# Table casts moved from VectorE to GpSimd, and a third group of keys put ahead of the quantiser's maximum

## The chip, the cores and the metric

The kernel runs on one core of a Trainium2 chip. Its five engines work side by side, each through its own instructions in order, and wait for each other by semaphores: TensorE (PE: matmuls and transposes; PEld is its loading of weights), VectorE (DVE), ScalarE (ACT), GpSimd (POOL) and SyncE (SP, which here only issues transfers). The metric is the device time of one execution in microseconds (us). Before the change it is 1597.74 us, the median of three runs (1596.93 to 1598.61).

## The reference

The program is two layers of a transformer on `x` of shape (2, 2048, 512), with a context of 128 tokens per batch, all in float32. Each layer is a cross attention and a feed-forward, both behind a normalisation and both added to `x`:

```python
x = x + _L0_xattn_ref(_layernorm(x), ctx_1024, ctx_1024, mask_BxS2_bf0, ...)
x = x + _L0_ffn_ref(_layernorm(x), clip_x, clip_down, w_gate, w_up, w_down)
x = x + _L1_xattn_ref(_layernorm(x), ctx_1024, ctx_1024, mask_1x1xSxS2_bk0, Wq, bq, Wk, bk, ...)
x = x + _L1_ffn_ref(_layernorm(x), Wg, bg, We, be)
```

The change lies where the first feed-forward begins. That feed-forward quantises its input with a single step for the whole tensor, and the step needs the largest absolute value over all tokens:

```python
def _act_fake_quant(x, clip_factor):
    scale = jax.nn.sigmoid(clip_factor) * jnp.max(jnp.abs(x)) / QMAX
    return jnp.clip(_ste_round(x / scale), -QMAX - 1.0, QMAX) * scale

xq = _act_fake_quant(x, clip_x[0])
gate = jnp.einsum('bsh,ih->bsi', xq, _weight_fake_quant(w_gate))
up = jnp.einsum('bsh,ih->bsi', xq, _weight_fake_quant(w_up))
h = _act_fake_quant(jax.nn.silu(gate) * up, clip_down[0])
return jnp.einsum('bsi,hi->bsh', h, _weight_fake_quant(w_down))
```

So no row of the feed-forward can be quantised before the attention has finished its last tile. The second attention projects keys and values from the context alone (`K = k @ Wk.T + bk`), so its keys don't depend on `x` and can be computed at any time. Its queries are `Q = q @ Wq.T + bq`, divided by the square root of the head's width. The second feed-forward is a mixture of eight experts, where each token goes to the one expert that its gate picks.

## The kernel before

The 4096 tokens are 32 tiles of 128 tokens (`NT`), one tile per SBUF buffer `x0` to `x31`, which hold the residual from beginning to end.

The first attention walks blocks of 256 tokens, with the order of the work on TensorE, VectorE, ScalarE and GpSimd written out by hand. At its end `finished` (line 456) adds a tile's attention to the residual, takes the mean and variance and has GpSimd raise the variance to the power of -0.5 (`rsqrt_eps`, line 101), which gives `rstd1`; `largest` (line 464) normalises the tile with it (`xn`, line 104) and takes the largest absolute value per row (line 468). The last two tiles, 30 and 31, go through this in sequence, and the maximum of tile 31 is the last thing that the quantiser waits for.

From line 572 on TensorE's order alone is kept as written; VectorE, ScalarE, GpSimd and SyncE are put in order by a planner that works with its own costs, so that instructions of this stage can come between the last ones of the attention. The planner's queue per engine is then fixed, and each engine runs it strictly in order.

The seam, lines 593 to 717, does these things:

- `table` (line 593) makes small tables of ascending numbers for the routing of the experts at the very end: GpSimd writes integers with `iota` into a shared buffer `ti`, and line 598 casts them into the table's own type. Five tables, of 8, 128, 24, 32 and 1 numbers per partition, go through the one buffer `ti`, each waiting for the cast of the one before. Beside them stand the fills of `before`, `onesb` and the first row of `cum`, and a select on GpSimd that makes `before` triangular.
- `keys` (line 658) computes one of four groups of the second attention's keys: four matmuls of `wk1` and the turned context into PSUM (two passes each in the profile, so eight records per group), and ScalarE's copy with the bias. `psm` has two PSUM buffers for this stage.
- `act_step` (line 620) makes the quantiser's step: VectorE's maximum `m` and its spread `mb`, TensorE's transpose `pm` (line 628), VectorE's `gm`, then `step`, `inv` and the scales `gsc`, `rsx`, `usc`.
- `quantised_x` (line 694) writes a tile as int8 (`xi`) and casts it to bf16 (`xq`); there are two buffers for the first and four for the second. `turned_x` (line 700) turns the first four tiles with TensorE's transposes (`ptx`) and ScalarE's copies, and all later ones with transposing DMAs on SyncE's queue.
- Lines 716 and 717 fill `ones1` (read by nobody) and divide the query bias `bq`; lines 720 to 736 load and combine rows for the gate's bias (`vrow`, `wrow`, `rowadd`), and GpSimd adds `rowadd` to the gate's weights at line 736.

The feed-forward (line 738) then runs eight blocks of 512 tokens by eleven slices of the hidden width. A slice is four matmuls into `pg` and four into `pu`, `gate` on ScalarE, the product `h` (line 752) and its maximum `hmax` (line 754) on VectorE, and the store of `h` to DRAM on SyncE (line 755). `pg` and `pu` have three PSUM buffers each, so TensorE starts the fourth `pu` when the first `h` is done. The tiles of the next block are quantised and turned along the way.

After that the down projection (lines 1211 to 1230) takes tile by tile: a matmul group `py`, VectorE's product `y`, and GpSimd's addition into the residual (line 813). The query bias is read at line 875, from the 25th of these iterations on.

Of the kernel before, what the change touches and what calls it, by code (L numbers as in the profile page):

```python
# [19 lines left out]
ALU = mybir.AluOpType  # L20
# [6 lines left out]
ND = D // P  # L27
# [6 lines left out]
H1, DH1 = 16, 32  # L34
# [29 lines left out]
def two_layers(ctx: ExitStack, tc: tile.TileContext, a, out):  # L64
    nc = tc.nc
# [85 lines left out]
    with ExitStack() as l0:  # L151
# [96 lines left out]
        def keys(g):  # L248

            pk = psm.tile([P, 2, B * T], F32, name="pk", tag="m")  # L250
            for par in range(2):
                for c in range(ND):
                    nc.tensor.matmul(
                        pk[:, par, :], wk[g][c // 2][:, c % 2, par, :], kvT[c // 2][:, c % 2, :], start=(c == 0), stop=(c == ND - 1)
                    )
            t = []
            for k, (par, tab) in enumerate(((0, cosk), (1, sink), (1, cosk), (0, sink))):
                t.append(turns_k[k // 2][:, k % 2])
                nc.vector.tensor_tensor(
                    t[k], pk[:, par, :].rearrange("p (b k) -> p b k", b=B),  # L260
                    tab.unsqueeze(1).to_broadcast([P, B, T]), ALU.mult,
                )
            nc.gpsimd.tensor_tensor(kTe[:, g, :].rearrange("p (b k) -> p b k", b=B), t[0], t[1], ALU.subtract)
            nc.gpsimd.tensor_tensor(kTo[:, g, :].rearrange("p (b k) -> p b k", b=B), t[2], t[3], ALU.add)
# [42 lines left out]
        def down(w, j):  # L307
            wb = quantised(w, sd[:, j : j + 1])

            def turn():  # L310
                nc.sync.dma_start(out=wdT[:, :, j * P : (j + 1) * P], in_=wb, transpose=True)

            return turn
# [14 lines left out]
        def normed(k):  # L328


            stats[k] = small.tile([P, NB0, 2], F32, name="stat")
            for t, n in enumerate(tiles[k]):
                mv = variance(xs[n])
                ve = small.tile([P, 1], F32, name="ve")
                nc.vector.tensor_scalar(ve, mv[:, 1:2], 1.0 + EPS, EPS * EPS, ALU.mult, ALU.add)
                nc.vector.tensor_copy(stats[k][:, t, 0:1], mv[:, 0:1])
                nc.gpsimd.tensor_tensor(stats[k][:, t, 1:2], ve, minus_half, ALU.pow)
            if k > 1:
                features_in(k)
                turned_in(k)  # L340
# [42 lines left out]
        def queries(u, par):  # L383

            k, g = divmod(u, NG)
            j, b = blocks[k]
            if par == 0:
                if j not in tabs:
                    tables_in(j)
                ropes[u] = [mid.tile([P, B0], F32, name=f"rt{i}", bufs=1) for i in range(4)]  # L390
            pq, rt = psm.tile([P, B0], F32, name="pq", tag="m"), ropes[u]
            for c in range(ND):
                nc.tensor.matmul(  # L393
                    pq, wqs[c // 2][:, c % 2, par, g * P : (g + 1) * P], xnTs[k][:, c, :], start=(c == 0), stop=(c == ND - 1)
                )
            cos, sin = tabs[j]
            if par == 0:
                nc.vector.tensor_tensor(rt[0], pq, cos, ALU.mult)  # L398
                nc.vector.tensor_tensor(rt[1], pq, sin, ALU.mult)
                return  # L400
            qs[u] = [mid.tile([P, B0], F32, name=f"q{i}") for i in range(2)]
            nc.vector.tensor_tensor(rt[2], pq, sin, ALU.mult)  # L402
            nc.gpsimd.tensor_tensor(qs[u][0], rt[0], rt[2], ALU.subtract)  # L403
            nc.vector.tensor_tensor(rt[3], pq, cos, ALU.mult)
            nc.gpsimd.tensor_tensor(qs[u][1], rt[3], rt[1], ALU.add)
# [181 lines left out]
    bq = wa.tile([P, ND], F32, name="bq")  # L587
    bob = wa.tile([P, D], F32, name="bob")
    masks = wa.tile([P, TPB, T], U8, name="masks")
    ones1 = wa.tile([P, DH1], F32, name="ones1")  # L590


    def table(shape, pattern, base=0, channel=0, dtype=BF16):
        ti = w1.tile([P, *shape], I32, name="ti", tag="ti")
        nc.gpsimd.iota(ti, pattern=pattern, base=base, channel_multiplier=channel)
        t = w1.tile([P, *shape], dtype, name=f"t{len(tables)}")
        tables.append(t)
        nc.vector.tensor_copy(t, ti)
        return t

    tables = []
    iota_e = table([NE], [[1, NE]], dtype=F32)
    iota_s = table([P], [[1, P]])
    iota_j = table([NJB], [[1, NJB]], dtype=F32)
# [1 line left out]
    iota_p = table([1], [[0, 1]], channel=1, dtype=F32)  # L606

    before = w1.tile([P, P], BF16, name="before")
    nc.vector.memset(before, 1.0)
    nc.gpsimd.affine_select(  # L610
        out=before, in_=before, pattern=[[1, P]], compare_op=ALU.is_ge, fill=0.0, base=-1, channel_multiplier=-1
    )
    onesb = w1.tile([P, P], BF16, name="onesb")
    nc.vector.memset(onesb, 1.0)
    hot = w1.tile([P, NT, NE], BF16, name="hot")

    cum = w1.tile([P, NT + 1, NE], BF16, name="cum")
    nc.vector.memset(cum[:, 0, :], 0.0)

    def act_step(psum, name, column_maxima):  # L620

        m = small.tile([P, 1], F32, name="m")
        nc.vector.tensor_reduce(m, column_maxima, AX.X, ALU.max)

        mb = small.tile([P, P], F32, name="mb", bufs=1)
        nc.vector.tensor_copy(mb, m.to_broadcast([P, P]))
        pm = psum.tile([P, P], F32, name="pm", tag="m")
        nc.tensor.transpose(pm, mb, ident)
        gm = small.tile([P, 1], F32, name="gm")
        nc.vector.tensor_reduce(gm, pm, AX.X, ALU.max)  # L630
        step = const.tile([P, 1], F32, name=f"step_{name}")
        nc.vector.tensor_scalar(step, gm, kept[name], 1.0 / QMAX, ALU.mult, ALU.mult)
        inv = const.tile([P, 1], F32, name=f"inv_{name}")
        nc.vector.reciprocal(inv, step)
        return step, inv

    with ExitStack() as up:
# [38 lines left out]

            return rest

        for f in range(2):
            keys(f)  # L680
        sx, isx = act_step(psm, "L0_ffn_clip_x", amax1)
        for f in range(2, ND):
            keys(f)
        rsx = kv.tile([P, NT], F32, name="rsx")
        nc.vector.tensor_scalar(rsx, rstd1, isx, None, ALU.mult)
        gsc = kv.tile([P, NI], F32, name="gsc")
# [13 lines left out]
        def turned_x(n):  # L700
            blk, t = divmod(n, NBF)
            if t == 0:
                xqTs[blk] = work.tile([P, ND, BF], BF16, name="xqT", bufs=2)
            if blk > 0:
                nc.sync.dma_start(out=xqTs[blk][:, :, t * P : (t + 1) * P], in_=xqs[n], transpose=True)
                return
            pt = psm.tile([P, ND, P], BF16, name="ptx", tag="m")
            for c in range(ND):
                nc.tensor.transpose(pt[:, c, :], xqs[n][:, c * P : (c + 1) * P], identb)
            nc.scalar.copy(xqTs[blk][:, :, t * P : (t + 1) * P], pt)  # L710
# [2 lines left out]
            quantised_x(n)  # L713
        for n in range(NBF):
            turned_x(n)
        nc.vector.memset(ones1, 1.0)
        nc.vector.tensor_scalar(bq, bq, 1.0 / math.sqrt(DH1), None, ALU.mult)


        nq = (NE + 1) * ND  # L720
# [17 lines left out]
        for blk in range(NT // NBF):  # L738
            for i in range(NI):
# [19 lines left out]
                t, odd = divmod(i, 2)  # L759
                n = (blk + 1) * NBF + t  # L760
# [3 lines left out]
                if i >= 3 and i % 2 == 1:  # L764
                    n = (blk + 1) * NBF + (i - 3) // 2
# [27 lines left out]
    def rounded(n):  # L793

        if 0 < n < NT:
            h = work.tile([P, NI, P], F32, name="hq", bufs=3)
            load(h, h_dram[n])
            his[n] = work.tile([P, NI, P], I8, name="hi")
            nc.scalar.activation(his[n], h, AF.Identity, scale=ish)

    def widened(n):
        if n < NT:
            hbs[n] = work.tile([P, NI, P], BF16, name="hb")
            nc.vector.tensor_copy(hbs[n], his[n])
# [49 lines left out]
    def turned1(n):  # L854

        blk, t = divmod(n, NB1)
        if t == 0:
            xTs[blk] = big.tile([P, ND, B1], F32, name="xT1")
        dst = xTs[blk][:, :, t * P : (t + 1) * P]
        if n >= TURNED:  # L860
            joined(dst, xn1s[n])
        else:
            nc.scalar.copy(dst, transposed(psm, xn1s[n]))
# [347 lines left out]
    for n in range(NT - held):  # L1211
        rounded(n + 2)
        widened(n + 1)
        for rest in rests:
            rest()
        down(n)
        rests = []
        if n == NT - held - 6:
            rests = [normed(t) for t in range(NB1)]
        if n == NT - held - 5:  # L1220
            for t in range(NB1):
                turned1(t)
        if n >= NT - held - 4:
            f = n - NT + held + 4
            queries(0, range(f, f + 1))
        if n == NT - held - 2:
            rests = [normed(NB1 + t) for t in range(NB1)]
        if n == NT - held - 1:
            for t in range(NB1):
                turned1(NB1 + t)  # L1230
# [5 lines left out]
    for n in range(NT):  # L1236
        blk, t = n // NB1, n % NB1
# [138 lines left out]
```

## Time and profile before

| What | Value |
|---|---|
| median of three runs | 1597.74 us (1596.93 to 1598.61) |
| the profiled execution's own time | 1599.43 us |
| its span, first to last instruction | 1597.4 us |
| TensorE busy | 1551.3 us, 97% of the span |
| VectorE, ScalarE, GpSimd busy | 75%, 45%, 37% |
| mean granted clock of TensorE | 0.995 |

Busy shares alone don't say what the seam costs, as it is 12 us of 1597. What does is the order of its instructions in time and the idle times between them. In the rows of the timeline the first number is the start in us from the span's beginning, the second the duration; then come the engine, the line, the operation with what it writes and reads, the shape, and the number of instructions; in brackets stand the engine's idle time just before and what ended it. In the table of waits the numbers behind the colon are the total in us, how often, and the longest.

By such rows the seam lies between 673 us, when the last tile's attention is added, and 686.5 us, when the first `pg` starts; the feed-forward's first two blocks end at about 726 us.

### The profile page before, as it was taken

The page shows a single profiled execution, that of the slowest core. Times are in us where ns is not written, and L with a number is a line of the kernel's source. Part 1 is how long each engine was busy: PE and PEld are TensorE (multiplying, and loading weights), DVE is VectorE, ACT ScalarE, POOL GpSimd, SP SyncE. Part 2 cuts the span into 40 slices and gives each one's busy share as a digit, 9 for nine tenths or more (in the row PEclk, how much of TensorE's full clock was granted, in tenths as well). Part 3 has the DMA queues.
Part 4 walks back from the last instruction along what each step waited for, and adds up shares of the span by engine and source line. Part 5 has one row for each costly group of instructions (what it writes and reads, how often), then busy time and mean ns, then how long its engine had stood idle before and what let it go on. Part 6 is the DMA issues. An engine that isn't in the chain of part 4 may idle for free. (4 is left out here: it accounts for less than half of the span.)

```text
span 1597.4 us, 26167 instructions
## 1 busy us (share of the span) xinstructions
PE 1551.3 (97%) x9542; PEld 909.1 (57%) x9542; DVE 1192.5 (75%) x2333; ACT 720.4 (45%) x1537; POOL 586.8 (37%) x580
## 2 busy tenths in 40 slices
PE   7999999999999999999999999999999999999997
PEld 5655555555555555544444466666666666654443
DVE  3467777777777886589986678888888888877442
ACT  1222222222222222243335566777777776763442
POOL 2232222222222222110005654555565444544553
PEclk9999999999999999999999999999999999999999
DMA  9511212111111220367768734221311111114553
GB/s 321 188 37 41 47 40 47 40 47 40 51 46 41 59 60 1 117 169 205 179 173 278 271 132 143 48 47 34 55 45 36 41 28 41 41 47 131 162 162 89
DMA packets 180571, 150.90 MB, mean 94 GB/s; under 512 B 97089, under 2 KB 144665, under 8 KB 180444
## 3 DMA queue, kind: packets, MB, share of 16 engines
q1 hardware_dynamic: 170188, 127.25, 28.5%
q0 software_dynamic: 6240, 18.70, 3.8%
q10 hardware_dynamic: 4016, 3.29, 0.9%
q8 instruction: 76, 1.25, 0.3%
q14 instruction: 51, 0.42, 0.1%
HBM read 89.97 MB, written 41.79 MB: 82 GB/s over the span
## 5 line engine op out<-in xcount | busy, mean ns | idle before, releaser
L419 ACT ACTIVATE pr<-sc 128x1024 f32<-128x1024 f32 x64 | 65.6, 1024 | 421.6 <-PE sc L414 421.4
L393 PE MATMUL pq<-xnT,wq 128*128 128x256 f32 x1024 | 254.4, 391 | 0.0
L451 PE MATMUL pw<-wo,att 128*128 128x512 f32 x512 | 230.8, 593 | 0.0
L393 PEld LDWEIGHTS pq<-xnT,wq 128*128 128x128 f32 x1024 | 184.4, 189 | 67.1 <-issue 44.0
L914 ACT ACTIVATE s<-s,mx 128x128 f32<-128x128 f32 x512 | 175.3, 388 | 28.1 <-DVE mx L905 28.1
L923 POOL TENSOR_TENSOR s<-s,rs 128x1024 f32<-128x1024 f32 x64 | 120.9, 1903 | 149.6 <-DVE rs L922 149.1
L403 POOL TENSOR_TENSOR q<-rt,rt 128x256 f32<-128x256 f32 x64 | 46.7, 730 | 339.7 <-DVE rt L402 335.2
L451 PEld LDWEIGHTS pw<-wo,att 128*128 128x128 f32 x512 | 96.9, 190 | 96.4 <-issue 89.9
L441 DVE RECIPROCAL rd<-sc 128x256 f32<-128x256 f32 x64 | 112.4, 1757 | 46.5 <-PE sc L435 46.5
L1195 PE MATMUL pz<-we,x 128*128 x312 | 139.3, 598 | 1.8 <-ACT x L832 1.6
L872 PE MATMUL pq<-xT,wq 128*128 128x256 f32 x512 | 122.6, 382 | 0.0
L978 PE MATMUL pl<-wgate,xnT 128*128 128x512 f32 x256 | 116.7, 599 | 0.0
L955 PE MATMUL pw<-wo,oT 128*128 128x512 f32 x256 | 115.2, 592 | 0.7 <-ACT oT L946 0.7
L872 PEld LDWEIGHTS pq<-xT,wq 128*128 128x128 f32 x512 | 96.0, 190 | 33.1 <-issue 20.3
L398 DVE TENSOR_TENSOR rt<-pq,rope_cos 128x256 f32<-128x256 f32 x64 | 27.0, 422 | 104.2 <-PE pq L393 104.2
L749 ACT ACTIVATE gate<-pg,gsc 128x512 f32<-128x512 f32 x88 | 60.5, 687 | 93.9 <-PE pg L744 84.0
L1195 PEld LDWEIGHTS pz<-we,x 128*128 128x128 f32 x312 | 58.2, 192 | 68.4 <-issue 65.2
L92 DVE BATCH_NORM_STATS2 st<-x 128x6 f32<-128x512 f32 x130 | 89.4, 688 | 6.0 <-DMA x<-in_ctx 3.8
L744 PE MATMUL pu<-xqT,wuT 128*128 128x512 bf16 x352 | 90.3, 379 | 2.6 <-DVE h L752 2.4
L744 PE MATMUL pg<-xqT,wgT 128*128 128x512 bf16 x352 | 90.3, 379 | 0.0
L900 DVE SCALAR_TENSOR_TENSOR s<-sc,keep 128x1024 f32<-128x1024 f32 x64 | 78.1, 1220 | 14.3 <-PE sc L892 9.1
L955 PEld LDWEIGHTS pw<-wo,oT 128*128 128x128 f32 x256 | 48.6, 190 | 55.3 <-issue 53.6
(226 smaller groups left out, 2811.8 us busy)
## 6 DMA issues: line engine op xcount, KB each, us to landing
h_dram<-h SPq DMA_DIRECT2D x88, 256.0 KB
hq<-h_dram SPq DMA_DIRECT2D x31, 704.0 KB
x_dram<-x SPq DMA_DIRECT2D x32, 258.0 KB
x<-in_x SPq DMA_DIRECT2D x32, 256.0 KB
we<-in_L_ffn_We SPq DMA_DIRECT2D x8, 1024.0 KB
xnT<-in_x_turned SPq DMA_DIRECT2D x14, 512.0 KB
along<-stat_dram SPq DMA_DIRECT2D x14, 256.0 KB
w_in<-in_L_ffn_w_gate SPq DMA_DIRECT2D x11, 256.0 KB
```

The lines of the kernel that those rows point to most:

```text
L92: nc.vector.bn_stats(out=st, in_=x)
L393: nc.tensor.matmul(pq, wqs[c // 2][:, c % 2, par, g * P : (g + 1) * P], xnTs[k][:, c, :], start=(c == 0), stop=(c == ND - 1))
L441: nc.vector.reciprocal(rd, sc[:, 0, B0:])
L451: nc.tensor.matmul(pw, atts[u][:, f, t * P : (t + 1) * P], wo[:, 2 * g + f, :], start=(g == 0 and f == 0), stop=(g == NG - 1 and f == 1),)
L744: nc.tensor.matmul(dst, w[:, c, i * P : (i + 1) * P], xqTs[blk][:, c, :], start=(c == 0), stop=(c == ND - 1),)
L872: nc.tensor.matmul(pq, wq1[:, c, f * P : (f + 1) * P], xTs[blk][:, c, :], start=(c == 0), stop=(c == ND - 1))
L900: nc.vector.scalar_tensor_tensor(s, sc[:, 2 * half : 2 * half + 2].rearrange("p r c k -> p (r c) k"), -MASKED, keeps[n].unsqueeze(1).to_br ...
L914: nc.scalar.activation(s[:, h, :], s[:, h, :], AF.Exp, bias=mx[:, h : h + 1], **accum)
L923: nc.gpsimd.tensor_tensor(s, s, rs.unsqueeze(2).to_broadcast([P, 8, T]), ALU.mult)
L955: nc.tensor.matmul(pw, os_[n][:, c, :], wo1[:, c, :], start=(c == 0), stop=(c == ND - 1))
L978: nc.tensor.matmul(pl, xn2T[n][:, c, :], wgate[:, c, :], start=(c == 0), stop=(c == ND - 1))
L1195: nc.tensor.matmul(pz, ring[j][:, c, :], we[:, bass.ds(e, 1), c, :], start=(c == 0), stop=(c == ND - 1))
```

## The change

Five casts of the tables, the three fills (`before`, `onesb`, `cum`) move from VectorE to GpSimd. The fill of `ones1` and the scaling of `bq` move from VectorE at the seam to GpSimd, behind the first tile of the down projection. The third group of keys moves ahead of the quantiser's maximum on TensorE, where two groups stood; one is left behind it. What is computed doesn't change.

```diff
@@ -595,7 +595,7 @@
         nc.gpsimd.iota(ti, pattern=pattern, base=base, channel_multiplier=channel)
         t = w1.tile([P, *shape], dtype, name=f"t{len(tables)}")
         tables.append(t)
-        nc.vector.tensor_copy(t, ti)
+        nc.gpsimd.tensor_copy(t, ti)
         return t
@@ -606,16 +606,16 @@
     before = w1.tile([P, P], BF16, name="before")
-    nc.vector.memset(before, 1.0)
+    nc.gpsimd.memset(before, 1.0)
     nc.gpsimd.affine_select(
         out=before, in_=before, pattern=[[1, P]], compare_op=ALU.is_ge, fill=0.0, base=-1, channel_multiplier=-1
     )
     onesb = w1.tile([P, P], BF16, name="onesb")
-    nc.vector.memset(onesb, 1.0)
+    nc.gpsimd.memset(onesb, 1.0)
     hot = w1.tile([P, NT, NE], BF16, name="hot")
 
     cum = w1.tile([P, NT + 1, NE], BF16, name="cum")
-    nc.vector.memset(cum[:, 0, :], 0.0)
+    nc.gpsimd.memset(cum[:, 0, :], 0.0)
@@ -676,11 +676,10 @@
-        for f in range(2):
+        for f in range(3):
             keys(f)
         sx, isx = act_step(psm, "L0_ffn_clip_x", amax1)
-        for f in range(2, ND):
-            keys(f)
+        keys(3)
@@ -713,8 +712,6 @@
         for n in range(NBF):
             turned_x(n)
-        nc.vector.memset(ones1, 1.0)
-        nc.vector.tensor_scalar(bq, bq, 1.0 / math.sqrt(DH1), None, ALU.mult)
@@ -1215,6 +1212,9 @@
         down(n)
         rests = []
+        if n == 0:
+            nc.gpsimd.memset(ones1, 1.0)
+            nc.gpsimd.tensor_scalar(bq, bq, 1.0 / math.sqrt(DH1), None, ALU.mult)
         if n == NT - held - 6:
             rests = [normed(t) for t in range(NB1)]
```

Where the planner puts the moved instructions, as the changed kernel is built: on GpSimd the first iota and the fill of `before` stand ahead of the `rstd` of tile 30; then come the cast of 8, the fill of `onesb`, the iota of 128, the select, the cast of 128, the fill of `cum`, and iota and cast of 24, 32 and 1; and only behind them the `rstd` of tile 31. On VectorE the cast `xq` of tile 8 moves ahead of the first `h`, and the next steps of quantising move one `h` back. On SyncE the load of `rowadd` falls behind the store of the third `h`. ScalarE's order stays.

## The prediction

> **What bounds the kernel now.** I read the page first, for what limits the whole; then the waits between 672 and 850 us, which hold the seam and the feed-forward; then the timeline there; last the groups of GpSimd by shape, because the change puts new kinds of work on it.
>
> ```profile
> span 1597.4 us, 26167 instructions
> PE 1551.3 (97%) x9542; PEld 909.1 (57%) x9542; DVE 1192.5 (75%) x2333; ACT 720.4 (45%) x1537; POOL 586.8 (37%) x580
> ```
>
> TensorE is busy 97% of the span, so only its idle time is to be had, here what it waits for at the seam and behind it:
>
> ```profile
> PE pu L744 <- DVE h L752: 2.4, 3, 1.4
> DVE vrow L730 <- DMA vrow<-in_L_ffn_bg: 2.3, 1, 2.3
> PE pm L628 <- DVE bq L717: 1.7, 1, 1.7
> ```
>
> The columns are the total, the times and the longest. The whole price of the seam's wait is 1.7 us, 0.1% of the span; 2.4 us more is lost in the first two blocks of the feed-forward, where VectorE is late with `h`. The timeline shows both in order:
>
> ```profile
> 674.35 3.62 PE L661 MATMUL pk<-ctxT,wq 128*128 128x256 f32 x16
> 674.80 0.56 POOL L101 TENSOR_TENSOR rstd<-ve,minus_half 128x1 f32<-128x1 f32 x1 [15.16 <-DVE ve L100]
> 676.63 0.78 POOL L101 TENSOR_TENSOR rstd<-ve,minus_half 128x1 f32<-128x1 f32 x1 [0.21 <-DVE ve L100]
> 677.76 0.54 DVE L104 TENSOR_SCALAR xn<-x,mean,rstd 128x512 f32<-128x512 f32 x1
> 679.65 0.30 PE L628 MATMUL pm<-ident,mb 128*128 128x128 f32 x1 [1.68 <-DVE bq L717]
> 686.48 1.03 PE L744 MATMUL pg<-xqT,wgT 128*128 128x512 bf16 x4
> 686.57 0.22 DVE L730 TENSOR_SCALAR vrow<-vrow 36x128 f32<-36x128 f32 x1 [2.27 <-DMA vrow<-in_L_ffn_bg]
> 700.03 1.40 DVE L104 TENSOR_SCALAR xi<-x,mean,rsx 128x512 int8<-128x512 f32 x1
> 702.60 1.46 DVE L698 CAST xq<-xi 128x512 bf16<-128x512 int8 x1
> 705.37 1.02 PE L744 MATMUL pu<-xqT,wuT 128*128 128x512 bf16 x4 [0.59 <-DVE h L752]
> 715.52 1.02 PE L744 MATMUL pu<-xqT,wuT 128*128 128x512 bf16 x4 [1.36 <-DVE h L752]
> 723.38 1.02 PE L744 MATMUL pu<-xqT,wuT 128*128 128x512 bf16 x4 [0.49 <-DVE h L752]
> ```
>
> Two `rstd` on GpSimd (tiles 30 and 31) release the last `xn`, whose maximum leads to `pm`. VectorE then idles 2.27 us for a transfer until 686.57; that transfer was issued at 684.58 behind megabytes of weights and waits for none of the seam's arithmetic. The columns in brackets are idle time and its end.
>
> ```profile
> L1004 POOL TENSOR_TENSOR cum<-cum,hot 128x8 bf16<-128x8 bf16 x32 | 20.2, 633 | 66.2 <-DVE keep L882 54.4 <-DVE x L1005 7.7 <-DVE hot L1003 4.1
> L1100 POOL TENSOR_SCALAR x<-x 128x176 f32<-128x176 f32 x1 | 0.7, 668 | 3.7 <-DVE x L1099 3.7
> L610 POOL TENSOR_SCALAR_AFFINE_SELECT before<-before 128x128 bf16<-128x128 bf16 x1 | 0.3, 294 | 0.0
> L595 POOL IOTA ti<- 128x128 int32 x1 | 0.2, 241 | 0.1
> ```
>
> GpSimd has no cast in this trace; these rows (mean ns behind the bar) bound one from both sides.
>
> **The change, part by part.** *Leaving VectorE.* Five casts (0.16, 0.20, 0.17, 0.17, 0.15), four fills (0.17, 0.17, 0.06, 0.09) and the bias (0.16) go: 1.50 us of busy time. Little of it lies on the chain: 0.10 between the last addition's end and the statistics at 675.45, and 0.13 ahead of `xn` at 677.76. The bias at 679.42 starts when `mb` is already running, and `pm` needs `mb` alone.
>
> *Joining GpSimd.* The built order is what matters: on GpSimd everything from the first cast to the last now stands between `rstd` of tile 30 and `rstd` of tile 31, and the queue is in order. Before, only two iotas and a select stood there. The fill of `before` and the first iota come ahead of tile 30, in 15.16 us of idleness: nothing. Behind it, from 675.36 (674.80 + 0.56): iotas 0.24 + 0.15 + 0.15 + 0.13, the select 0.29, the fills of `onesb` 0.21 and `cum` 0.10 by the fills at the kernel's start, 1.27 in all. Five casts: at least what an iota of the same shape takes (0.82 together), at most what small arithmetic takes (0.65 each by L1004 and L1100, 3.25). I take 0.3 each, 1.5, by the select, the nearest row with one input. Five of them wait on the one just before; gaps of 0.1 stand before the dependent L1101 to L1103, so 0.5. Sum 3.3 (2.6 to 5.0). So `rstd` of tile 31 starts at 678.65 and not 676.63, takes 0.67 (mean of the two rows), and `xn`, 0.1 later, starts at 679.4 against 677.76: **+1.65 us (+0.95 to +3.35)**. The 0.23 saved on VectorE is inside this wait and is worth nothing. `pm` moves from 679.65 to 681.3 (680.6 to 683.0).
>
> The Trainium skill (GPSIMD Engine Reference, section 4.1 Engine selection) speaks against the move for two-input work, about twice as slow, and puts one-input work at roughly line rate. The trace agrees on the first: the same 128x512 addition takes 1.27 at L675 on GpSimd and 0.68 at L459 on VectorE. By its second half the casts would cost 0.85 as on VectorE, and `xn` would move by +1.0.
>
> *The third group of keys.* Eight matmuls (half of the 3.62, 1.81) move ahead of `pm`: TensorE is busy to 679.78, then idles until 681.3, 1.5 us (0.8 to 3.2) against 1.68. Behind `pm`, one group is left instead of two. Before, the transposes started 3.4 after `pm` behind keys; now the first waits for `xq` (ready 2.7 after `pm`), and what ends last is ScalarE's four copies of 2.21 in all and the second pair of `xq`, 4.65 after `pm`. The first `pg` then stands 6.45 behind `pm` instead of 6.83: **-0.38**. It starts at 687.75, **+1.27 (+0.55 to +2.95)** against 686.48.
>
> *What covers it.* VectorE ends the fourth `xq` at 681.3 + 4.65 = 685.95, still before the transfer at 686.57. So its later work starts when it did; at the upper end (687.65) it is 1.1 late. TensorE, 1.27 behind, then meets 0.59 + 1.36 + 0.49 = 2.44 us of stalls on `h` that VectorE and the transposing transfers time, and they shrink by as much. The seam's delay is thus paid out of stalls and not out of the end. Were this cover gone, the cost would be 1.27.
>
> *VectorE's order in the first block.* `xq` of tile 8 moves ahead of the first `h` (+0.33 of issue for `h`); its buffer is freed by a transpose issued at 688.10, and the like one issued at 709.22 let its cast start 2.6 later, so 690.7 against 691.15: no wait. Three later steps move back by one `h`. The two slow rows at 700.03 and 702.60 take 1.40 and 1.46 where the same forms take 0.53 and 0.41, while GpSimd's L736 runs; by the new order each should start about half a microsecond later into that. I take -0.3 for VectorE, between -0.6 and +0.6.
>
> *Queues.* On SyncE the load of `rowadd` falls behind the store of the third `h`; it was waiting 1.5 us for `v_dram` until 696.45, and that store is issued by 695.4: nothing. The late fill and bias on GpSimd stand ahead of tile 1's addition, 0.10 + 0.65 in an idle time of 1.75; the bias is read 24 tiles on: nothing, or 0.75 of GpSimd alone if that slack is gone.
>
> *Clock.* Three stretches of the span (stretch, length, TensorE's busy time first, the granted clock before the last two columns):
>
> ```profile
> 957.80:961.20 3.40, 1.43 (x12) 0.95 (x11) 2.48 (x6) 2.06 (x4) 2.72 (x3) 1.00 1.05 389
> 961.20:964.60 3.40, 3.40 (x39) 2.59 (x40) 2.87 (x7) 1.15 (x2) 0.38 (x1) 0.50 1.04 386
> 678.00:681.30 3.30, 1.65 (x8) 1.50 (x9) 2.75 (x13) 0.48 (x1) 0.01 (x1) 1.00 0.89 295
> ```
>
> After a stretch with 1.43 of 3.40 busy the next ran at a granted 0.50. The seam, with 1.65 of 3.30, is followed by 1.00: on the edge. A halving costs up to 1.7 of TensorE's work, first out of the same stalls; I count none, and keep it for the range. The Trainium skill (TensorE: Matmul & The Clock Gate, section Why this matters for your kernels) warns of idle gaps over some 3 us; the longest single gap before the drop here is 1.72. By its rule the likeliest case has no drop, and neither does my sum.
>
> **Sum.** On the profiled execution (1599.43, its span 1597.4 and 2.0 around it) the end moves by -0.3, to 1599.1. That execution stands 1.69 above the median of 1597.74, so the forecast is **1597.4 us**. Two tenths of a per cent, 3.2 us, is about what a measurement of this kernel can tell from no change.
>
> **The rivals.** *Slower: GpSimd's queue outgrows its cover.* It decides where `xn` is more than 2.27 late, for then VectorE starts late too. With casts at 0.65 TensorE idles 3.2, a halving (+1.7) is likely, and 2.95 + 1.7 - 2.44 = +2.2 gives 1599.9; with 1.0 each it is +4.0, 1601.7. For it: arithmetic rows of GpSimd cost over 0.5 however small. Against: fills, iotas and the select don't.
>
> *Faster: the stalls go as well.* Casts at iota's price (+0.55 at `pg`), VectorE clear of L736 and the transposes landing sooner: 0.55 - 2.44 = -1.9, 1595.8; with one clock drop fewer of three in the run, 1594.1. For it: VectorE has 1.5 us less to do. Against: the 1.36 us stall follows a transfer (`xq` idles 1.54 at 714.38), not VectorE's work.
>
> *Hidden anyway.* VectorE's order gains nothing, and the end is 1597.7.
>
> **How the numbers follow.** Likeliest 0.45, hidden 0.28, slower 0.17 (some 0.14 of it past 3.2 us, clock included), faster 0.10 (0.08 past it). That gives 0.08, 0.78 and 0.14. The likeliest and the hidden case alone span 1596.5 to 1598.8, the runs' own spread included. The range reaches to -1.9 with half a microsecond of spread, 1595.2, and to the slower rival between 0.65 and 0.85 a cast, 1600.7.
>
> **What would show it.** In the new profile `rstd` of tile 31 stands behind five casts on GpSimd and starts near 678.7, counted as here; `pm` still waits 1 to 2 us; `vrow` still waits for its transfer, but less than 1 us; `pg` starts 0.5 to 3 us later; the stalls of `pu` on `h` are under 1.5 us in all. It is wrong if a cast on GpSimd takes over 0.85 us, if the clock drops at the seam, or if the stalls on `h` stay at 2.4 with `pg` late.

## The result and the profile after

The changed kernel takes **1600.77 us** (1597.23 to 1604.11, 22 runs) beside 1598.43 us (1596.26 to 1601.69, 22 runs) of the kernel before on the same chip: a ratio of **1.0013**, with a 95% interval of 1.0007 to 1.0018. Three repeats gave 1.0006 (0.9996 to 1.0016), 1.0015 (1.0006 to 1.0024) and 1.0017 (1.0005 to 1.0029). Weighted by runs, the mean of the times is 2.2 us later. The forecast was 1597.4 us and no change, with a range up to 1600.7; what came is a small loss, just beyond that end.

The page of the changed kernel:

```profile
span 1601.5 us, 26170 instructions
PE 1553.6 (97%) x9542; PEld 907.7 (57%) x9542; DVE 1192.8 (74%) x2323; ACT 719.6 (45%) x1537; POOL 586.6 (37%) x590
```

VectorE lost ten instructions and GpSimd gained ten (2333 to 2323, 580 to 590), but VectorE's busy time is the same. The waits between 672 and 850 us, TensorE's:

```profile
PE ptx L708 <- DVE xq L697: 1.6, 2, 0.8
PE pu L741 <- DVE h L749: 1.2, 1, 1.2
PE pm L628 <- DVE mb L626: 0.7, 1, 0.7
```

The wait before `pm` fell from 1.7 to 0.7 us because the third group of keys fills it, and the stalls of `pu` on `h` from 2.4 to 1.2. The timeline of the seam:

```profile
674.98 0.56 POOL L101 TENSOR_TENSOR rstd<-ve,minus_half 128x1 f32<-128x1 f32 x1 [15.01 <-DVE ve L100]
676.23 0.31 POOL L598 CAST t<-ti 128x128 bf16<-128x128 int32 x1
676.82 0.38 POOL L598 CAST t<-ti 128x24 f32<-128x24 int32 x1
678.11 0.56 POOL L101 TENSOR_TENSOR rstd<-ve,minus_half 128x1 f32<-128x1 f32 x1
678.71 0.55 DVE L104 TENSOR_SCALAR xn<-x,mean,rstd 128x512 f32<-128x512 f32 x1 [0.85 <-POOL rstd L101]
680.60 0.30 PE L628 MATMUL pm<-ident,mb 128*128 128x128 f32 x1 [0.73 <-DVE mb L626]
687.25 0.22 DVE L727 TENSOR_SCALAR vrow<-vrow 36x128 f32<-36x128 f32 x1 [2.00 <-DMA vrow<-in_L_ffn_bg]
687.91 1.52 PE L741 MATMUL pg<-xqT,wgT 128*128 128x512 bf16 x4
716.50 1.02 PE L741 MATMUL pu<-xqT,wuT 128*128 128x512 bf16 x4 [1.17 <-DVE h L749]
```

The five casts (0.21, 0.31, 0.38, 0.21, 0.19) stand between the two `rstd`, as forecast. The first `pg` takes 1.52 us instead of 1.03. The stretches around it say why (TensorE's busy time first, granted clock third from the end):

```profile
682.10:685.50 3.40, 1.79 (x19) 1.00 (x17) 3.15 (x8) 1.64 (x4) 0.00 (x0) 1.00 1.09 310
685.50:688.90 3.40, 3.15 (x9) 1.11 (x7) 1.65 (x5) 2.27 (x3) 0.00 (x0) 0.50 0.12 29
```

The clock was halved for 3.4 us behind a stretch in which TensorE was busy 1.79 of 3.40 us. But the feed-forward, which ended at 841.81 before, ends at 842.39 here: +0.58, of which 0.18 is the first key group's own later start (674.35 to 674.53). So in this one execution nearly all of the 4.1 us by which its span is longer comes later, and one pair of profiles can't say what of it belongs to the change. The prediction also had `vrow` waiting less than 1 us; it waits 2.00 here, as VectorE came to it earlier than reckoned and the transfer later. The eighteen runs below are also eighteen more profiles; the table of all stands behind them.

### The profile page after: what moved, and what is told of

Same layout as the page of the kernel before. It is cut to its first block, busy times and chain, and to the rows that moved or that the text cites. A ratio compares the mean times of both kernels' runs of the same rounds, so it can differ in the third digit from the quotient of the medians.

```text
span 1601.5 us, 26170 instructions
## 1 busy us (share of the span) xinstructions
PE 1553.6 (97%) x9542; PEld 907.7 (57%) x9542; DVE 1192.8 (74%) x2323; ACT 719.6 (45%) x1537; POOL 586.6 (37%) x590
## 3 DMA queue, kind: packets, MB, share of 16 engines
q8 instruction: 76, 1.25, 0.3%
## 5 line engine op out<-in xcount | busy, mean ns | idle before, releaser
L807 PE MATMUL py<-wdT,hb 128*128 128x512 bf16 x352 | 79.7, 385 | 3.5 <-DVE hb L801 2.8
```

Source lines behind the costliest of these rows:

```text
L807: nc.tensor.matmul(py, hbs[n][:, i, :], wdT[:, i, :], start=(i == 0), stop=(i == NI - 1))
```

## The experiments

Each computes the whole result; what is added is read by nobody. "Before" and "after" are the two kernels. Ratios are to the kernel before on the same chip, with 95% intervals.

**The three parts, one at a time.** `keys_only` is before with the third group of keys moved:

```diff
-        for f in range(2):
+        for f in range(3):
             keys(f)
         sx, isx = act_step(psm, "L0_ffn_clip_x", amax1)
-        for f in range(2, ND):
-            keys(f)
+        keys(3)
```

> Only the third group of keys moves ahead of the maximum; casts, fills and bias stay on VectorE. Queue theory (the casts on GpSimd hold up rstd of tile 31 and so pm): no change here, pm at 679.7 +-0.2 and the total within 0.7 us of before. Clock theory (the group was work that kept TensorE busy behind pm; without it the stretch behind pm is half idle and the next 3.4 us run at a granted 0.50): slower by 1 to 2 us, with 0.50 between 681 and 689 in the profile. Late-stage theory (the bias on GpSimd, or what follows it, costs the time in the down projection): no change.

Measured: 1.0038 (1.0026 to 1.0051), some 6 us slower, which none of the three theories had. In the order that the planner gave this kernel, VectorE's `vrow` stands ahead of the `inv` that the quantiser needs. VectorE's timeline, and a stretch of the same time:

```profile
687.03 0.22 DVE L729 TENSOR_SCALAR vrow<-vrow 36x128 f32<-36x128 f32 x1 [5.85 <-DMA vrow<-in_L_ffn_bg]
687.17 0.15 DVE L634 RECIPROCAL inv_L_ffn_clip_x<-step_L_ffn_clip_x 128x1 f32<-128x1 f32 x1
```

```profile
686.00:689.40 3.40, 0.37 (x4) 0.37 (x5) 2.37 (x10) 0.00 (x0) 0.00 (x0) 0.50 0.07 21
```

An in-order engine waits 5.85 us for a transfer while the step of the quantiser stands behind it. The first `pg` starts at 693.77. TensorE starves meanwhile, and its clock is halved from 686.0 to 696.2. So the parts don't add up: in the full change the same edit goes with another order.

`tables_only` is before with the casts and fills on GpSimd (lines 598 to 618); `bias_only` has `ones1` and `bq` on GpSimd in the down projection.

> Only the casts and fills go to GpSimd; two groups of keys ahead of the maximum, bias on VectorE at the seam. Queue theory: pm about 0.95 late as in the changed kernel, pg 0.9 late, the total slower by 0.5 to 2.3 us. Clock theory: TensorE's wait before pm grows to 2.6 us, and the granted clock falls there too, slower by 1 to 2; without a fall in the profile within 0.7. Late-stage theory: no change.

> Only the fill and the query bias move to GpSimd behind the first tile of the down projection. Queue theory and clock theory: within 0.7 us of before. Late-stage theory: slower by 1.5 to 2.3 us, with more waits of py for hb between 850 and 905.

Measured: 1.0006 (0.9997 to 1.0014) and 1.0004 (0.9995 to 1.0012), neither clear of no change. With the tables alone `pm` comes 0.78 later net of the first keys' start, and the idle time before it is longer, since nothing fills it:

```profile
680.61 0.30 PE L628 MATMUL pm<-ident,mb 128*128 128x128 f32 x1 [2.46 <-DVE bq L717]
```

The clock halves at 681.8, the first `pg` is 2.46 us later than before and not 0.9 as expected, and still the feed-forward ends no later (167.01 us after the first keys, 167.46 before): TensorE doesn't wait for `h` at all there. This is the cover of the prediction at work.

`tables_late` is after with the iotas written into the buffer `mb` of `act_step` (`spread[0]` below) and the table block moved behind `turned_x`, so that the iotas and casts on GpSimd must come behind `pm` and the second `rstd`:

```diff
-        ti = w1.tile([P, *shape], I32, name="ti", tag="ti")
+        ti = spread[0][:, : shape[0]].bitcast(I32)
```

> The changed kernel, but the integers are made in the buffer of the spread maximum (mb), so that iotas and casts come on GpSimd behind pm and behind rstd of tile 31; three fills and the select stay ahead of it. Queue theory: pm back at 679.5 to 679.9 and the total back within 0.7 us of before, or up to 0.5 faster. Clock theory: the layout of the keys is the changed kernel's, so still 1 to 2 us slower with 0.50 behind the seam. Late-stage theory: still 2.3 us slower.

Measured: 1.0015 (1.0005 to 1.0026). `pm` stands at 679.07 with the first keys at 673.39 (+0.38 net), the first `pg` is level (+0.08), the clock isn't halved at the seam, and the loss is there (its `vrow` is late all the same, as the table will show). Only the select and the fill of `cum` are left between the two `rstd`, and the second one waits for VectorE. So casts ahead of the second `rstd` aren't needed for a loss in the median.

`tables_bias` is after with two groups of keys ahead, as before:

> The changed kernel with two groups of keys ahead of the maximum instead of three; tables and bias on GpSimd as in the change. Theory A (the loss of 0.13% belongs to the new place of the third group of keys, which the changed kernel and the one with late tables have in common): ratio to the kernel before at or below 1.0005, some 1598.5 to 1599.5 us beside 1598.4. Theory B (the loss belongs to the tables and the bias together, or to no part: clock drops and transfers after 842 us): ratio 1.0010 to 1.0015. In both, pm starts near 680.6 and TensorE idles longer behind it than in the changed kernel, since the keys no longer fill the time before pm; a clock drop near 682 us in about two of three executions.

Measured: 1.0001 (0.9991 to 1.0012); a second run of after on the same chip gave 1.0006. The interval holds both theories. The clock drop came where it was expected, at 681.2.

**What chance does.** Unaltered copies:

> The kernel before a second time, unaltered: what the comparison itself can tell, and a second profile. Ratio 0.9995 to 1.0005 by every theory. If drops of the clock are drawn anew in each execution, they are not at 961.2, 1333.3 and 1480.1 again; if they belong to the kernel, they are.

> The kernel before a third time: ratio 0.9994 to 1.0006 by every theory; its profile's stages show how far chance alone moves them: up to 2 us each.

> The changed kernel a second time, unaltered, for a second profile beside the next run. Theory A (the drops of the granted clock are drawn anew in each execution, by where a grid of 3.4 us falls on the idle gaps): the profile has drops at other places than 685.5, 914.2 and 965.4, or fewer, each worth 1.6 to 1.9 us, and the stage from 850 to 947 us is shorter by 1.7 if the drop at 914 is missing. Theory B (they belong to this kernel): the same three drops. Ratio to the kernel before 1.0007 to 1.0018 in both.

> The changed kernel a third time. Theory A (the change costs something that is always there): ratio 1.0008 to 1.0018. Theory B (what it costs is small beside the stages' chance): ratio anywhere between 0.9998 and 1.0016, and the profile's stages differ from those of the first two by up to 2 us each without an order. The feed-forward ends within 0.6 us of the kernel before, counted from the first keys, in both.

> The changed kernel a fourth time, beside the two above on the same chip: ratio to the kernel before 1.0007 to 1.0016, the code load 1.0 to 1.7 us behind the last pid matmul, last stage 180.5 to 183 us.

Measured: the two of before 1.0000 (0.9989 to 1.0011) and 1.0001 (0.9991 to 1.0011), the three of after as given at the top. The last stage of `after_fourth` took 180.11 us, a little under what was expected. The clock drops lie elsewhere in each: none in the first repeat of after, three in the second (913.3, 964.5, 1336.6). So they are drawn anew, and their price can be read: from the last `py` to the first expert the twelve profiles without a drop near 962 take 463.8 to 464.2 us, the eight with one 465.4 to 465.8: 1.6 us. The stage ahead of it, up to the last `py`, takes 100.9 to 102.5 us in the thirteen profiles without a drop near 914 and 102.6 to 104.7 in the seven with one.

**Filling the idle gaps.** `after_fill` (and `fill_again`, the same kernel) puts eight unread matmuls of 256 to 512 columns (the expectation miscounts them as nine) into six of TensorE's gaps between 910 and 1334 us; `fill` is empty elsewhere:

```diff
+        for q in fill:
+            nc.tensor.matmul(pt.rearrange("p c q -> p (c q)")[:, :q], ident, wo1[:, 0, :q], start=True, stop=True)
         for c in range(n):
             nc.tensor.transpose(pt[:, c, :], src[:, c * P : (c + 1) * P], ident)
```

> The changed kernel with nine matmuls more whose results nobody reads, put into TensorE's idle gaps near 912, 959, 961 and 1335 us (0.4 to 1.35 us each gap, of gaps of 0.76 to 1.95); nothing else moves. If halved clock after half-idle stretches is what costs: these gaps lead to 1.5 drops per execution of 1.6 to 1.9 us each, so the time falls by 2.5 us against the changed kernel, ratio to the kernel before 0.9990 to 1.0002, and the profile has no drop near 914, 962 or 1337. If the drops cost nothing, or do not follow from the gaps: the same ratio as the changed kernel, 1.0007 to 1.0018, or more by up to 0.3 us where a filler outlasts its gap.

> The changed kernel with nine unread matmuls in four idle gaps, a second time, beside the changed kernel on the same chip. If clock drops behind those gaps cost: 1.5 to 2.5 us less than the changed kernel, ratio to the kernel before lower by 0.0010 to 0.0016. If not: the same as the changed kernel within 0.0006.

The gap near 912, of the profile after and then of `after_fill`:

```profile
910.80:914.20 3.40, 1.62 (x11) 1.14 (x12) 3.37 (x7) 0.86 (x2) 1.59 (x3) 1.00 0.93 323
914.20:917.60 3.40, 3.40 (x10) 1.20 (x9) 0.38 (x1) 1.68 (x2) 1.51 (x1) 0.50 0.31 104
```

```profile
910.80:914.20 3.40, 2.73 (x14) 1.58 (x13) 3.33 (x8) 0.57 (x1) 1.61 (x2) 1.00 0.86 313
914.20:917.60 3.40, 3.35 (x17) 2.08 (x16) 1.68 (x3) 1.96 (x3) 2.02 (x2) 1.00 0.35 109
```

Neither profile has a drop at the filled gaps; of the four profiles of after without fillers three have two or three there. The ratios are 1.0005 (0.9996 to 1.0014) and 1.0004 (0.9995 to 1.0013), beside 1.0006 and 1.0015 of after on the same chips. In the first pair the gain is nil, in the second it is 0.11%; the expectation of the first, 0.9990 to 1.0002, was missed. `before_fill` does the same to before:

> The kernel before with the eight unread matmuls in TensorE's idle gaps near 910, 957, 961 and 1330 us. Clock account: drops behind these gaps cost what the three comparisons of the changed kernel with and without the matmuls show, 0.0005 to 0.0011, in the kernel before as well: ratio 0.9989 to 0.9996, no drop between 900 and 1340. Rival (the matmuls help only what the change has hurt): 0.9998 to 1.0004.

Measured: 0.9999 (0.9989 to 1.0008), again without a drop between 900 and 1340; the point is where the rival had it, and the interval holds both. `fill_pad` below against `dve_pad` is 0.08% again. What the fillers are worth is somewhere between nothing and 0.1%; the runs don't say more, and no version here is shown to beat the kernel before.

**Instructions counted instead of timed.** In the profiles so far the last stage (first to last expert matmul) took up to 182.8 us with the tables on GpSimd and at most 180.0 with them on VectorE. `pool_pad` adds eleven fills on GpSimd to before, near the start, where it idles:

> The kernel before with eleven fills of a scratch column on GpSimd in its idle time of 4.7 us near 1.4 us; nothing reads them. The profiles so far have a last stage (first expert matmul to the last matmul) of 178.6 to 180.0 us in the four kernels with the tables on VectorE and of 178.7 to 182.8 in the six with the tables on GpSimd. Theory A (that is the count of instructions ahead on GpSimd, so the place of its code loads): the last stage takes over 181 us here, ratio 1.0005 to 1.0015. Theory B (that is chance, in the transposing transfers ahead of the experts): the last stage anywhere between 178.6 and 182.8, ratio 0.9993 to 1.0007.

Measured: 1.0008 (0.9999 to 1.0016), last stage 179.55 us, not over 181: the count on GpSimd alone doesn't lengthen it. What does go with it is VectorE's. The engines' code comes in transfers of its own, and one of 8 KB that runs 5.9 to 7.8 us ahead of the last `pid` matmul (the routing of the experts, line 1142 before and 1139 after) in all kernels that leave VectorE its instructions or take two, runs 1.0 to 1.7 us behind it in all that take eight or ten away (times from that matmul's end). GpSimd's scatter is in flight there, and its next one waits for it. GpSimd's timeline of a repeat of before and of after:

```profile
1479.58 1.89 POOL L1200 DMA_INDIRECT out_x<-x,x  x1 [1.03 <-DVE x L1134]
1483.99 1.02 POOL L1200 DMA_INDIRECT out_x<-x,x  x1 [1.16 <-DVE x L1148]
```

```profile
1479.57 1.91 POOL L1197 DMA_INDIRECT out_x<-x,x  x1 [1.01 <-DVE x L1131]
1485.14 1.02 POOL L1197 DMA_INDIRECT out_x<-x,x  x1 [2.30 <-DMA out_x<-x,x]
```

The same two scatters are 4.41 us apart and 5.57. The third scatter shows less of it: it starts 7.3 us behind the last `pid` matmul on average in the ten profiles with the load ahead, and 7.7 in the ten with it behind. `dve_pad` is after with ten fills on VectorE in the down projection; `before_less` is before with ten fills of a column of `x` moved from VectorE to GpSimd in the second attention, and nothing of the change:

```diff
+        if 0 < n < 11:
+            nc.vector.memset(spare[:, n - 1 : n], 0.0)
```

```diff
-        nc.vector.memset(xw[n][:, D + 3 : D + 4], 0.0)
+        (nc.gpsimd if n < 10 else nc.vector).memset(xw[n][:, D + 3 : D + 4], 0.0)
```

> The changed kernel with ten fills of a scratch column on VectorE in the down projection, where VectorE idles 0.88 us per tile; nothing reads them. They put VectorE's number of instructions ahead of the last stage back to that of the kernel before. Theory A (the loss comes from VectorE's code load, which in all eight profiles with the tables on GpSimd starts 1.0 to 1.7 us behind the last pid matmul, and in the six others 5.9 to 7.7 us ahead of it): the load starts 6 to 8 us ahead of the last pid matmul, the second scatter of out_x behind it comes 2.9 to 3.0 us after that matmul and not 3.6 to 4.2, the last stage takes 178.6 to 180.0 us and not 181 to 183, and the ratio to the kernel before is 0.9995 to 1.0006. Theory B (the load's place is only a bystander): the load is back, but the last stage stays over 181 us and the ratio at 1.0008 to 1.0016.

> The kernel before, nothing of the change in it, with the fill of one column of x in ten tiles of the second attention moved from VectorE to GpSimd. VectorE has ten instructions fewer ahead of the last stage, as in the changed kernel. Theory A (VectorE's code load): it starts 1 to 2 us behind the last pid matmul, the second scatter comes at 3.6 to 4.2 us, the last stage takes 180.5 to 183 us, the ratio is 1.0005 to 1.0016, with the seam as in the kernel before. Theory B (bystander): last stage 178.6 to 180, ratio 0.9995 to 1.0005.

The second scatter in `dve_pad`, and in `before_less`:

```profile
1481.26 1.90 POOL L1198 DMA_INDIRECT out_x<-x,x  x1 [1.02 <-DVE x L1132]
1485.72 1.02 POOL L1198 DMA_INDIRECT out_x<-x,x  x1 [1.20 <-DVE x L1146]
```

```profile
1480.33 1.89 POOL L1200 DMA_INDIRECT out_x<-x,x  x1 [1.02 <-DVE x L1134]
1485.89 1.08 POOL L1200 DMA_INDIRECT out_x<-x,x  x1 [2.31 <-DMA out_x<-x,x]
```

The local part is shown from both sides: put VectorE's ten instructions back and the load lies 7.6 us ahead, the scatters 4.46 apart; take ten away from the old kernel and it lies 1.2 behind, the scatters 5.56 apart. Whether the time follows is not shown: `before_less` seems to lose (1.0011, with an interval from 1.0000 to 1.0021), but `dve_pad` gets nothing back that is clear of noise (1.0013, 1.0003 to 1.0024; after on the same chip 1.0017). Two more go further: `fill_pad` is `dve_pad` with the eight unread matmuls, and `turn_pad` is `dve_pad` with 117 fills on GpSimd, meant to move GpSimd on by one whole code load (the expectation counts eleven instructions from the change, the profile ten):

```diff
+        for _ in range(5 if n < 5 else 4):
+            nc.gpsimd.memset(spare2, 0.0)
```

> The changed kernel with both: the unread matmuls in TensorE's idle gaps near 912, 959, 961 and 1335 us, and the ten fills on VectorE. If both accounts hold (1.9 us for the code load, 1 to 2.5 us for the clock drops behind these gaps) it is faster than both kernels: ratio to the kernel before 0.9983 to 0.9996, last stage 178.6 to 180 us, no drop between 900 and 1340. If only the load's: 0.9996 to 1.0006. If neither: 1.0004, as without the fills.

> The changed kernel with ten unread fills on VectorE and 117 on GpSimd (four or five per tile of the down projection). A code load brings 8 KB; VectorE is back at its number of instructions, and GpSimd, which the change gives eleven more, is 128 ahead, which is one load of 64-byte instructions: every later load should fall where it falls in the kernel before (13 to 15 us ahead of the last pid matmul, 7.5 us ahead of it, 84 us behind it). Theory A (the loss is due to the places of the code loads, of both engines together): ratio to the kernel before 0.9996 to 1.0006. Theory B (it is not): 1.0008 to 1.0017 as the changed kernel, or more if the fills cost time themselves; the loads are back all the same.

Measured: `fill_pad` 1.0005 (0.9995 to 1.0015), with a last stage of 181.56 us although VectorE's load is back, and `turn_pad` 1.0010 (1.0001 to 1.0019). In `turn_pad` all three loads of the last stage are back (13.2 and 7.8 us ahead, 84.0 behind) and the stage takes 178.89 us, and still the kernel is slower than before. So the last stage isn't the whole loss, and the theory that the code loads there are the cause falls as stated.

**All profiles side by side** (without `keys_only`, where another order rules: first `pg` 18.76, end 173.37). Times in us, from the traces: first the start of VectorE's `vrow`, of the first `pg` and the end of the feed-forward, each counted from the first key matmul; then the three stages behind (to the last `py`, on to the first expert, on to the last expert matmul).

| Profile | vrow | pg | FF end | to last py | to expert | last stage |
|---|---|---|---|---|---|---|
| before | 12.22 | 12.13 | 167.46 | 101.44 | 465.53 | 178.61 |
| before_again | 12.65 | 12.13 | 167.23 | 101.64 | 465.46 | 179.99 |
| before_third | 12.14 | 12.13 | 166.53 | 103.66 | 463.97 | 179.25 |
| bias_only | 12.20 | 12.12 | 166.25 | 101.18 | 463.83 | 178.91 |
| pool_pad | 12.51 | 12.13 | 166.97 | 102.48 | 465.51 | 179.55 |
| before_less | 12.23 | 12.12 | 166.80 | 103.26 | 463.85 | 180.88 |
| before_fill | 12.28 | 12.13 | 167.70 | 101.27 | 463.98 | 180.12 |
| tables_only | 12.43 | 14.59 | 167.01 | 102.00 | 465.40 | 182.19 |
| tables_bias | 12.65 | 14.59 | 167.70 | 101.74 | 463.88 | 181.48 |
| tables_late | 13.23 | 12.21 | 167.50 | 104.15 | 465.35 | 182.42 |
| after | 12.72 | 13.38 | 167.86 | 104.71 | 465.68 | 178.73 |
| after_again | 12.67 | 12.48 | 166.85 | 102.41 | 464.15 | 182.76 |
| after_third | 14.42 | 12.48 | 169.85 | 102.59 | 465.76 | 181.26 |
| after_fourth | 13.09 | 12.48 | 167.91 | 104.19 | 465.72 | 180.11 |
| dve_pad | 13.98 | 13.38 | 167.93 | 102.52 | 463.85 | 180.14 |
| turn_pad | 13.15 | 12.49 | 168.96 | 103.85 | 464.14 | 178.89 |
| after_fill | 14.27 | 13.38 | 169.56 | 101.69 | 464.16 | 181.05 |
| fill_again | 12.55 | 12.48 | 166.59 | 101.64 | 464.16 | 180.14 |
| fill_pad | 12.58 | 12.48 | 167.46 | 102.53 | 463.87 | 181.56 |

Read the first three columns. From the first keys the feed-forward's end moves over 3.6 us from row to row. It stands 153.95 to 155.81 us behind `vrow`, a spread of 1.9, and 152.42 to 157.37 behind `pg`, a spread of 5. No run moves `vrow` alone, and in before's seam, where `vrow` hardly moves, the two aren't visibly tied; so this is a correlation, carried by the late rows. What TensorE's waits add says it more directly: take from each row's end the start of `pg` and all waits of `pu` for `h`, and 152.4 to 153.6 us remain. In the seven kernels with before's seam `pg` stands at 12.13 and these waits come to 2.1 us on average, in the nine with after's at 12.78 and 2.2. The later `pg` was not paid for by shorter waits.

The seven kernels with before's seam have `vrow` at 12.32 and the end at 166.99 on average, the nine with after's seam at 13.27 and 168.11: **+0.95 and +1.12 us**. `vrow` waits for two transfers, and the second is issued later, by 0.8 us on average, because the issue of the first takes longer. SyncE's queue before and after:

```profile
677.53 7.00 SPq L75 DMA_DIRECT2D vrow<-in_L_ffn_be  x1
684.58 0.36 SPq L75 DMA_DIRECT2D vrow<-in_L_ffn_bg  x1
```

```profile
677.47 8.06 SPq L75 DMA_DIRECT2D vrow<-in_L_ffn_be  x1
685.58 0.36 SPq L75 DMA_DIRECT2D vrow<-in_L_ffn_bg  x1
```

The issue of the first `vrow` load takes 6.91 to 7.25 us in the eight profiles with the tables on VectorE and 7.45 to 8.35 us in the twelve with them on GpSimd, without an overlap. In eleven of those twelve, all that take ten instructions from VectorE ahead of the seam's end, a code load of 8 KB falls into this very time, 7.8 to 9.4 us after the first keys; in the other nine profiles it runs 5.7 to 6.0 us ahead of them. Among the transfers of 674 to 690 us of after stands the line

```profile
q14 instruction: 1, 0.01, 0.1%
```

and before has none on that queue there. In the second repeat of after the landing is later still, and TensorE is stalled already in the fourth slice, a stall that no kernel with before's seam has there:

```profile
688.58 0.22 DVE L727 TENSOR_SCALAR vrow<-vrow 36x128 f32<-36x128 f32 x1 [3.69 <-DMA vrow<-in_L_ffn_be]
694.47 1.02 PE L741 MATMUL pu<-xqT,wuT 128*128 128x512 bf16 x4 [1.61 <-DVE h L749]
```

That the code load is what delays the issue is not shown: `tables_only`, which takes only eight instructions from VectorE, has its load where before has it, and its issue takes 7.45. The fills of `dve_pad` and `turn_pad` stand behind the seam and left this load in its new place (9.2 and 7.8 after the first keys), so they couldn't mend it. Ten fills on VectorE ahead of the seam would tell; that was not tried.

## Why the prediction was wrong

*GpSimd's queue: right in kind, reckoned too dear.* The order is as read from the build. The second `rstd` starts at 678.11, not 678.65: the casts took 1.30 in all and not 1.5, and the instructions overlap a little instead of leaving gaps. The `rstd` took 0.56 and not 0.67. `pm` comes at 680.60; net of the first keys' start it is +0.77, under the range's lower end of 0.95. A cast on GpSimd costs about half as much again as on VectorE (1.30 against 0.85 for the five), where the Trainium skill (GPSIMD Engine Reference, section 4.1 Engine selection) has one-input work at roughly line rate; the rows decide.

*Third group of keys: right.* The first `pg` stands 6.41 behind `pm` in the repeats of after without a drop, 6.83 before: -0.42, forecast -0.38.

*Clock: the case that was left out.* Three of the nine profiles with after's seam have a drop there, none of the seven with before's, both of those with the tables moved and two groups ahead. It costs 0.90 at the first `pg` (13.38 against 12.48) and made the +1.27 of the forecast come out at +1.25 by accident; without it `pg` is 0.35 late.

*Cover: the step that failed.* "That transfer was issued at 684.58 behind megabytes of weights and waits for none of the seam's arithmetic", and so "its later work starts when it did". There is such a cover: 2.46 us of delay at the first `pg` vanish in `tables_only`, where `vrow` is hardly late (12.43); the 6.6 us of `keys_only` are too much for it. But I took the transfer's landing as fixed. `vrow` moved by 0.95 us on average (0.5 in the profiled pair). So the stalls on `h`, which were to "shrink by as much", stayed at 2.2 us beside 2.1, and the feed-forward's end moved by 1.12, where the sum has -0.3. That the late `vrow` kept them up is the likely reading, but no run moved it alone. A cover that is itself a wait must be asked what sets *its* end. The prediction looked at what the transfer waits for, not at what else goes over the same queues in that time.

*VectorE's order: the size was off.* VectorE reaches its first `h` 5.1 us behind `vrow` with after's order, 4.9 before: the `xq` that moved ahead costs 0.2, and the gain forecast for it isn't steady. The rows that run beside GpSimd's addition to the gate's weights (line 736 before) cost 1.92 us over their usual time before, 2.32 in after and 1.35 in its first repeat.

*Queues, late bias: right.* `bias_only` shows no effect that the comparison can see.

*What the sum didn't have at all.* It ended with the feed-forward. The last stage takes 179.33 us on average in the seven profiles whose code loads lie as before (`keys_only` among them), 181.10 in the ten with VectorE's load behind the routing (the three with only GpSimd's loads moved take 180.4): +1.8. Only the 1.1 between two scatters is shown, by `dve_pad` and `before_less`, and one scatter on 0.4 of it is left. How much of it reaches the median is open, since the runs with the load put back are no faster than the interval allows. With +1.1 from the feed-forward and clock drops of 1.6 each thrown by chance, the account could cover 2.2 us, but it is a sum of stage means with a spread of about 1 us each. What makes the whole loss stays open.

Of the rivals, "slower" has the right sign and the wrong place: GpSimd's queue never outgrew its cover. "Faster" asked for stalls on `h` to go; they fell to 1.2 us in one profile and rose to 4.3 in another of the same kernel.

## What to carry to other kernels

Where a delay is hidden behind a wait for a transfer, price the transfer too: ask what else is put on its queues, and compare its landing in several executions before taking it as fixed. At a tenth of a per cent a single pair of profiles proves nothing (the stages here move by 2 us by chance); a table by stage over many profiles showed what four comparisons of medians could not. An instruction moved between engines also moves later code loads of both, as the runs with ten fills more or fewer show.

## What the hardware showed that was not expected

- TensorE's clock is halved after a stretch of 3.4 us with TensorE busy too little, whether one gap makes it or several. Lay the grid of 3.41 us that the drops mark over each of the twenty profiles, between 30 and 1565 us. Of the stretches at full clock all 25 with less than 1.60 us busy are followed by a granted 0.50, and 7 of the 45 with 1.60 to 1.87; none above is. The grid shifts from execution to execution, so the same gap is punished in one and not in the next. The longest single gap before such a drop near 914 is 1.95 us. The Trainium skill (TensorE: Matmul & The Clock Gate, section HAM oscillation — how this bites in real kernels) speaks of idle gaps over some 3.4 us; here little more than half of that was enough. The drop near 962 costs 1.6 us.
- The engines' code is loaded by transfers of 8 and 16 KB all through the run, and one that falls on GpSimd's scatter delays the next by 1.1 us. Ten instructions more or fewer on VectorE shift it by 9 us there.
- Issuing one transfer of 16 KB behind full queues takes SyncE 6.91 to 7.25 us, and 7.45 to 8.35 with the tables on GpSimd; why is open.
